# Finding a token's experts by comparing logits, with routing, early tokens and weight pieces in another order: a recurrence with a mixture of experts

## The chip, the core and the metric

The kernel runs on one core of one Trainium2 chip. The metric is the device time of one execution in microseconds (us). Three runs of the kernel before gave 386.06, 385.2 and 385.53, a median of 385.53. What a chip measurement here can tell from no change is about 0.2% of that. "TensorE" is PE in the profile, "VectorE" DVE, "ScalarE" ACT, "GpSimd" POOL and "SyncE" SP.

## What is computed

Inputs are `x` (2 x 1024 x 256), a start state per sequence, the recurrence's weights, a gate of 8 experts and three weight matrices for each of them. In the module, a recurrence over 64-step segments, then a mixture of experts, are added to `x`:

```python
xW = jnp.einsum('ntd,dh->nth', x, Wx) + b
next_h = jnp.tanh(xw_t + prev_h @ Wh)          # step by step
...
logits = x_flat @ gate_w.T                     # 2048 tokens, 8 experts
top_v, top_i = jax.lax.top_k(logits, 2)
probs = softmax(top_v)
hidden = silu(x_flat @ wg[e].T) * (x_flat @ wu[e].T)
out += weight[e] * (hidden @ wd[e].T)          # every expert e
```

Only the two experts with the largest logits have a weight other than zero for a token, so the kernel computes those alone.

## The kernel before, in words

**Tokens.** The 2048 hidden states are held as 16 tiles of 128 tokens (`r` = 0 to 15). The recurrence is not run over 64 serial steps of two sequences but in a wide form, 128 columns in each of the steps `s` = 8 to 63 (lines 623 to 670), whose warm-up the last part of the run checks: `chunk_starts` (line 550) subtracts the states where two chunks meet, `starts_check` (684) turns the differences into a mark `okh`, and `starts_flag` (677) adds it up over the partitions. If the mark fails, `stepwise` (1024) computes everything again, step by step, behind a branch at the end of the kernel. Steps 48 to 63 each finish one token tile.

**A step of the recurrence.** TensorE does four fp32 products (line 630) onto an accumulator that was *seeded* two steps earlier with `x @ Wx + b` (`seed`, line 315: one half copied by VectorE, one by ScalarE for s of 50 and more), then ScalarE does two tanh.

**Routing.** It is interleaved with steps 49 to 63, by a list of due times: `at(t, f)` files `f` under a time and `run(t)` (lines 556 to 562) carries out, in order of due times, everything due. `run` is called in the middle of step `s` with `s - 0.5` (line 629) and at its end with `s` (670), then in the main loop with `64 + n` plus a fraction. Every engine executes what it is given in program order, so a due time is a place in the queue of each engine that the function uses. The tiles are routed in four groups (`GROUPS = (5, 3, 5, 3)`). For a tile, `route_tile` (360) has TensorE transpose the states to rows with the logits behind them and ScalarE copy them to SBUF; `route_max` (370) takes the eight largest logits and their indices on VectorE. For a group, in this order:

- `route_choice` (376): one-hot rows `oh` of the two experts by comparing a counter with the indices, their sum `sel`, and the difference `dl` of the two logits. `route_weight` (394): tanh of `dl` on ScalarE.
- `rows_out` (389): the rows go to a DRAM table `rows_d` by SyncE's DMA queue.
- `route_position` (399): TensorE counts with small fp16 products (line 408) how many earlier tokens chose each expert. It reads `sel`.
- `route_code` (412): VectorE turns the count into a slot number, split into `v` and `m`. GpSimd puts the expert weights into the rows (464, 465).
- `route_onehot` (435), in three parts: two one-hot matrices (parts 0 and 2) and a multiplication by the token number (part 1). In the trace their tile is called `wd`, since they lie in that buffer.
- `route_slots` (449): TensorE multiplies them (line 455), so that a table says for every slot of every expert which token stands in it.

`early_gap` (430) and `early_slots` (481) need groups 0 and 1 only: GpSimd gathers the first two tiles of expert 0's tokens from `rows_d` (line 469) while the recurrence still runs, and `early_turn` (492) transposes them (line 216), splits them into a high part `xhi` on ScalarE and a low part `xlo` on VectorE. `all_slots` (495) does the rest after group 3.

**Experts.** `jobs` are experts, `units` are up to 512 token columns of one. Each unit takes `NIC` = 8 steps, numbered `n` through all units. In step `n` (lines 937 to 974) `front` (837) has TensorE do 12 products, gate first, then up, each as high x high, low x high, high x low (`products`, 722); `gate` (858) does silu on ScalarE and the product on VectorE, then splits the hidden values; `back` of step `n - 2` (877) does the second matmul (line 892) into `yb`. After a unit's last `back`, ScalarE scales its rows into `y` and GpSimd scatters them with an add. `turn` (822) transposes and splits the next unit's tokens. Weights of the next expert are loaded in fp32 by SyncE (771) and split into two parts in six pieces (`piece`, 773; ScalarE for the high part, VectorE for the low), at the places that `split_at` lists (927 to 933). `expert_order` (504) sorts the experts in five portions, one at each `next(order_ops)`.

Of the kernel before, what the change touches and what calls it, by code (L numbers as in the profile page):

```python
# [8 lines left out]
F32 = mybir.dt.float32  # L9
# [3 lines left out]
U32 = mybir.dt.uint32  # L13
# [6 lines left out]
P = 128  # L20
# [4 lines left out]
E = 8  # L25
# [11 lines left out]
NA = 8  # L37
ET = 2
TOL = 2.0**-18


class Pools:
# [15 lines left out]
def rnn_moe(ctx, tc, xT, xrows, h0T, Wx, Wh, b, gw, W, out):  # L58
# [282 lines left out]
    gi5 = ov.tile([P, NO * NS], I32, name="gi5")  # L341
    si5 = ov.tile([P, NO * NS], I32, name="si5")
    gap = ov.tile([P, 1], F32, name="gap")
    eq = ov.tile([P, NO * NS], F32, name="eq")
    sel = ov.tile([P, R, E], F16, name="sel")
    hot_space = spare[1].bitcast(F16)
# [13 lines left out]
    def route_tile(gr, r):  # L360
        i = r - gr["r0"]
        if i == 0:
            gr["mx"] = rt.tile([P, gr["n"], 8], F32, name="mx")
            gr["mi"] = rt.tile([P, gr["n"], 8], U32, name="mi")
        pt = ptr_tile()[:, 0:ROW]
        for k in range(2):
            pe(nc.tensor.matmul(pt[:, k * P : (k + 1) * P + E], lhsT=hall[k][:, r, :], rhs=ig[:, k, :], start=(k == 0), stop=(k == 1), skip_group_check=True))  # L367
        act.copy(gr["rows"][:, i, :], pt)

    def route_max(gr, r):  # L370
        i = r - gr["r0"]
        lg = gr["rows"][:, i, P : P + E]
        vec.max(gr["mx"][:, i, :], lg)
        vec.max_index(gr["mi"][:, i, :], gr["mx"][:, i, :], lg)

    def route_choice(gr):
        n = gr["n"]
        gr["oh"] = oh = rt.tile([P, n, 2, E], F32, name="oh")
        vec.tensor_tensor(
            oh,  # L380
            iota_f[:, 0:E].unsqueeze(1).unsqueeze(1).to_broadcast([P, n, 2, E]),
            gr["mi"][:, :, 0:2].unsqueeze(3).to_broadcast([P, n, 2, E]),
            ALU.is_equal,
        )
        vec.tensor_tensor(sel[:, gr["r0"] : gr["r0"] + n, :], oh[:, :, 0, :], oh[:, :, 1, :], ALU.add)
        gr["dl"] = dl = rt.tile([P, n], F32, name="dl")
        vec.tensor_tensor(dl, gr["mx"][:, :, 1], gr["mx"][:, :, 0], ALU.subtract)

    def rows_out(gr, cs):
        a, b = gr["r0"] * P, (gr["r0"] + gr["n"]) * P  # L390
# [21 lines left out]
    def route_code(gr):  # L412
        n = gr["n"]
        rows = route_rows(gr)
        tmp = rt.tile([P, n, 2, E], F32, name="tmp")
        next(rows)
        vec.tensor_tensor(tmp, gr["oh"], pos_ps[:, 0:n, :].unsqueeze(2).to_broadcast([P, n, 2, E]), ALU.mult)
        code = rt.tile([P, n, 2], F32, name="code")
        next(rows, None)
        vec.tensor_reduce(code, tmp, AX.X, ALU.add)  # L420
        big = 1.5 * 2.0**23 * P
        vv = rt.tile([P, n, 2], F32, name="vv")
        vec.tensor_scalar(vv, code, 0.5 - P / 2, big, ALU.add, ALU.add)
        gr["v"] = v = rt.tile([P, 2 * n, 2], F16, name="v")
        twice = lambda t: t.rearrange("p i c -> p (i c)").unsqueeze(2).to_broadcast([P, 2 * n, 2])
        vec.tensor_scalar(v, twice(vv), -big, 1.0 / P, ALU.add, ALU.mult)
        gr["m"] = m = rt.tile([P, 2 * n, 2], F16, name="m")
        vec.scalar_tensor_tensor(m, v, -float(P), twice(code), ALU.mult, ALU.add)

# [126 lines left out]
    def at(step, f, *args):  # L556
        todo.setdefault(step, []).append(lambda: f(*args))

    def run(step):
        for t in sorted(t for t in todo if t <= step):  # L560
            for f in todo.pop(t):
                f()
# [8 lines left out]


    maxima = {r: r + 49.5 for r in range(R)}
    maxima.update({5: 55, 8: 58.2, 9: 59.2, 10: 60.3, 11: 61, 13: 62.3, 14: 63.2, 15: 64.13})
    for g, gr in enumerate(groups):
        for r in range(gr["r0"], gr["r0"] + gr["n"]):
            at(r + 49 if r < 15 else 64.1, route_tile, gr, r)
# [2 lines left out]
    def group(g, choice, weight, position, code, hot, slots):  # L580
        gr = groups[g]
        at(choice, route_choice, gr)
        at(weight, route_weight, gr)
        at(choice + 0.01, rows_out, gr, ((0, P), (P + E, ROW)))
        at(position, route_position, gr)
        at(code, route_code, gr)
        at(code, rows_out, gr, ((P, P + E),))
        for part, t in enumerate(hot):
            at(t, route_onehot, gr, part)
        for i in range(gr["n"]):  # L590
            at(slots, route_slots, gr, i)

    group(0, 53.5, 53.6, 54.5, 54.5, (54.6, 54.6, 55.1), 57.1)
    group(1, 56.5, 56.6, 57, 57, (57.1, 57.1, 57.1), 59)
    at(57.6, early_gap)
    at(59, early_slots)
    group(2, 61.5, 61.6, 62, 62, (62.4, 63.3, 64.2), 66.6)
    at(62.1, early_turn)
    group(3, 64.13, 64.14, 65.1, 65.13, (65.2, 66.2, 67.2), 67.6)
    at(67.6, all_slots)  # L600
    at(69.6, chunk_starts)

    inj = {}
# [80 lines left out]
    def starts_check():  # L684
        vec.tensor_tensor(df, df, df, ALU.mult)
        vec.tensor_scalar(df, df, TOL * TOL, None, ALU.is_le)
        vec.tensor_reduce(okm, df, AX.XYZ, ALU.min)
        vec.tensor_copy(okh, okm)

    def loop_tile(pool, rank, kth):  # L690

# [27 lines left out]
    with ExitStack() as c2:  # L719
        open_late_pools(c2)  # L720

        def products(lhs_rhs, pt=None):

            if pt is None:
                pt = pgu_tile()
            for i, j in ((0, 0), (1, 0), (0, 1)):
                for n, (a, b) in enumerate(lhs_rhs):
                    pe(nc.tensor.matmul(  # L728
                        pt, lhsT=a[i], rhs=b[j],
                        start=(i + j + n == 0), stop=(j == 1 and n == len(lhs_rhs) - 1), skip_group_check=True))  # L730
            return pt

        def gated(pg, pu, between=lambda: None):
# [52 lines left out]
        class Unit:  # L786
# [49 lines left out]

            def front(u, s, between=lambda: None):

                w, x = u.job.w, u.x
                if u.main:  # L840
                    c = slice(s * P, (s + 1) * P)
                    n = u.cols
                    if 2 * n <= 512:
                        t = pgu_tile()
                        pt = [t[:, 0:n], t[:, n : 2 * n]]
                    else:
                        pt = [pgu_tile()[:, 0:n] for _ in range(2)]
                    pairs = [[(pick(w[nm], k, c), pick(x, k, slice(0, n))) for k in range(2)] for nm in NAMES[:2]]
                    pg = products(pairs[0], pt[0])
                    between()  # L850
                    pu = products(pairs[1], pt[1])
                else:
                    c = slice(s * 512, (s + 1) * 512)
                    a = slice(0, P)
                    pg, pu = (products([(pick(x, k, a), pick(w[nm], k, c)) for k in range(2)]) for nm in NAMES[:2])
                u.hid[s] = pg, pu
# [70 lines left out]
        split_at = {}  # L927
        for j in range(len(jobs) - 1):
            two = sum(u.job is jobs[j] for u in units) > 1
            for n, m in enumerate((2, 3, 4, 6, 7) if not two else (8, 10, 12, 14, 15) if j == 0 else (3, 4, 7, 10, 12, 15)):  # L930
                split_at[j, m] = j + 1, n
            if j == 0 or not two:
                split_at[j + 1, 0] = j + 1, 5
# [3 lines left out]
        for n in range(len(steps)):  # L937
            i, s = steps[n]
            u = units[i]
            j = jobs.index(u.job)  # L940
            m = s + (NIC if i and units[i - 1].job is u.job else 0)
            u.front(s, lambda: run(64 + n + 0.1))
            run(64 + n + 0.15)
            low = []

            def beside():
                run(64 + n + 0.2)
                if (j, m) in split_at:
                    to, p = split_at.pop((j, m))
                    low.append(jobs[to].piece(p, jobs[to + 1] if to + 1 < len(jobs) else None))  # L950

            u.gate(s, beside)
            for f in low:
                f()
            run(64 + n + 0.3)
            if n == 16:
                starts_check()
            elif n == 20:
                next(order_ops, None)
                starts_flag(ptr_tile()[:, 0:1])  # L960

            if n == 4:
                units[1].gather()
                units[2].gather()
            if s == (6 if i == 0 else 5) and i + 1 < len(units):
                units[i + 1].turn()
            for _ in range({5: 1, 6: 1, 7: 2, 9: 1}.get(n, 0)):
                next(order_ops)
            if i > 0 and s == 2 and i + 2 < len(units):
                units[i + 2].gather()  # L970
            if 2 <= n < len(steps) - NIC + TAIL + 2:
                v, t = units[steps[n - 2][0]], steps[n - 2][1]
                v.back(t)
            run(64 + n + 0.6)
# [183 lines left out]
```

## Time and profile before

| | us |
|---|---|
| three runs, median | 385.53 (385.2 to 386.06) |
| the profiled execution, its own time | 389.46 |
| its span, first to last instruction | 387.3 |
| TensorE busy in the span | 369.7 |
| recurrence and routing: first expert product (line 728) starts | 76.82 |
| first unit's last step's products start | 94.47 |
| second expert's first products start | 115.74 |

The span is divided in the view by stages as follows (length of the stage, then busy us of each engine with instruction counts, granted TensorE clock, share of DMA, GB/s):

```
0.00:28.00 28.00, 26.71 (x228) 25.36 (x228) 21.14 (x79) 15.26 (x57) 19.39 (x38) 1.00 0.81 301
28.00:53.00 25.00, 23.42 (x169) 20.24 (x168) 15.86 (x49) 15.51 (x52) 0.37 (x9) 1.00 0.37 127
53.00:76.80 23.80, 22.20 (x227) 21.69 (x226) 16.19 (x95) 16.33 (x61) 3.89 (x8) 1.00 0.23 59
76.80:98.20 21.40, 19.45 (x180) 18.59 (x178) 14.57 (x53) 7.37 (x21) 6.40 (x8) 1.00 0.34 89
98.20:128.50 30.30, 29.13 (x210) 27.11 (x210) 22.14 (x47) 17.87 (x36) 12.15 (x10) 1.00 0.48 146
128.50:175.00 46.50, 46.50 (x325) 43.54 (x325) 28.34 (x52) 23.60 (x44) 20.34 (x16) 1.00 0.51 137
175.00:372.00 197.00, 196.70 (x1344) 187.48 (x1343) 108.29 (x194) 99.81 (x188) 48.02 (x32) 1.00 0.33 81
372.00:387.40 15.40, 5.62 (x48) 5.39 (x46) 0.00 (x0) 1.90 (x4) 6.10 (x4) 0.83 0.31 36
```

The columns of engines are PE, PEld (weight loads, beside PE), DVE, ACT and POOL. Almost all VectorE and ScalarE operations carry one line number (L54, the helper that records them), so they are told apart by their tiles. A bracket at the end of a timeline row is the idle time of that engine before the row, and after the arrow who ended it.

### The profile page before, as it was taken

To read this page: it belongs to the slowest core of one execution; us is meant where nothing else is said; L and a number is where in the kernel's file an instruction comes from. 1 tells how busy PE (TensorE), PEld (TensorE's weight loads), DVE (VectorE), ACT (ScalarE), POOL (GpSimd) and SP (SyncE) were. 2 spreads that over 40 slices of the span, in tenths; PEclk is the share of its full clock that TensorE was granted. 3 is DMA by queue.
4 is the path that set the end of the run, shared out by engine and by line. 5 is a ranking of instruction groups with operands and counts; after the bars stand their busy time and mean duration, and the time that the engine had idled before them with its cause. 6 is when DMAs were issued, how large, how long until landed. Compare 5 with 4: busy or idle time off the path is not lost.

```text
span 387.3 us, 7245 instructions
## 1 busy us (share of the span) xinstructions
PE 369.7 (95%) x2717; PEld 349.4 (90%) x2717; DVE 226.5 (58%) x567; ACT 197.6 (51%) x458; POOL 116.7 (30%) x124
## 2 busy tenths in 40 slices
PE   8999999989999899999999999999999999999990
PEld 8998898889997789999999999999989999999890
DVE  6876648684777566564546564566545655663410
ACT  3746666632564644645445644665454555444420
POOL 3780001206171510783223602523040014006042
PEclk9999999999999999999999999999999999999997
DMA  7952334133075534664246243445143144003113
GB/s 223 460 202 96 108 111 114 50 95 82 5 191 181 135 111 135 151 199 89 86 125 126 72 129 94 81 138 135 30 107 114 47 173 51 1 2 40 13 20 38
DMA packets 19227, 42.20 MB, mean 109 GB/s; under 512 B 4802, under 2 KB 14178, under 8 KB 16066
## 3 DMA queue, kind: packets, MB, share of 16 engines
q1 hardware_dynamic: 12402, 32.32, 24.1%
q0 software_dynamic: 6496, 9.09, 14.3%
q8 instruction: 23, 0.38, 0.4%
q10 hardware_dynamic: 288, 0.26, 0.2%
q14 instruction: 18, 0.15, 0.1%
HBM read 35.15 MB, written 9.14 MB: 114 GB/s over the span
## 4 chain that ended last, share of the span: by engine, by line
PE 85%; DVE 4%; ACT 3%; DMA 2%; POOL 2%; issue 2%; SPq 1%; POOLq 0%; ACTq 0%; DVEq 0%
PE pgu_t L728 46%; PE yb L892 22%; PE pgu_t L630 8%; PE ptr L309 3%; PE ptr L216 2%; POOL out_dram L476 2%; DVE wd L54 1%; DMA wh<-in_Wh_dram 1%; PE pgu_t L892 1%; DMA xg<-rows_d,gidx 1%; PE ptr L641 1%; ACT h L54 1%; PE ptr L367 1%; PE ptr L892 1%; DVE g L54 1%
## 5 line engine op out<-in xcount | busy, mean ns | idle before, releaser
L892 PE MATMUL yb<-wd,hh 128*128 128x256 f32 (+2 forms) x544 | 94.3, 284 | 1.5 <-ACT y L54 1.5
L54 DVE TENSOR_TENSOR g<-g,pgu_t 128x256 f32<-128x256 f32 (+5 forms) x96 | 50.2, 522 | 64.1 <-PE pgu_t L728 44.3
L892 PEld LDWEIGHTS yb<-wd,hh 128*128 128x128 f32 (+2 forms) x544 | 80.4, 185 | 3.8 <-ACT y L54 2.2
L54 ACT ACTIVATE g<-pgu_t 128x256 f32<-128x256 f32 (+5 forms) x96 | 44.9, 468 | 71.3 <-PE pgu_t L728 66.1
L476 POOL DMA_INDIRECT out_dram<-y,si x27 | 44.1, 1635 | 119.5 <-ACT y L54 114.0
L728 PE MATMUL pgu_t<-xhi,gu_g 128*128 128x256 f32 (+5 forms) x384 | 78.3, 325 | 0.8 <-ACT xhi L54 0.8
L54 ACT CAST hh<-g 128x256 fp32r<-128x256 f32 (+5 forms) x92 | 44.7, 486 | 65.2 <-DVE g L54 62.5
L728 PE MATMUL pgu_t<-xhi,gu_u 128*128 128x256 f32 (+5 forms) x384 | 78.0, 325 | 0.0
L728 PEld LDWEIGHTS pgu_t<-xhi,gu_u 128*128 128x128 f32 x384 | 61.3, 188 | 4.3
L728 PEld LDWEIGHTS pgu_t<-xhi,gu_g 128*128 128x128 f32 x384 | 58.7, 189 | 3.3 <-ACT xhi L54 1.0
L54 DVE TENSOR_TENSOR hl<-g,hh 128x480 fp32r<-128x480 f32 (+4 forms) x52 | 31.1, 597 | 32.1 <-ACT hh L54 31.4
L892 PE MATMUL yb<-wd,hl 128*128 128x256 f32 (+1 forms) x176 | 49.6, 282 | 0.0
L728 PE MATMUL pgu_t<-xlo,gu_g 128*128 128x256 f32 (+5 forms) x192 | 46.7, 324 | 0.0
L728 PE MATMUL pgu_t<-xlo,gu_u 128*128 128x256 f32 (+5 forms) x192 | 46.5, 323 | 0.0
L469 POOL DMA_INDIRECT xg<-rows_d,gi x27 | 29.3, 1084 | 47.8 <-DVE cm L819 18.8
L728 PEld LDWEIGHTS pgu_t<-xlo,gu_g 128*128 128x128 f32 x192 | 32.5, 188 | 2.5 <-DVE xlo L54 0.2
L728 PEld LDWEIGHTS pgu_t<-xlo,gu_u 128*128 128x128 f32 x192 | 32.5, 188 | 2.2
L892 PEld LDWEIGHTS yb<-wd,hl 128*128 128x128 f32 (+1 forms) x176 | 32.2, 183 | 0.1
L630 PE MATMUL pgu_t<-h,wh 128*128 128x128 f32 (+1 forms) x224 | 28.6, 266 | 1.4
L54 DVE TENSOR_TENSOR hh<-g,hh 128x256 fp32r<-128x256 f32 x40 | 17.0, 426 | 20.5 <-ACT hh L54 18.8
L54 ACT ACTIVATE h<-pgu_t 128x128 f32<-128x128 f32 (+1 forms) x72 | 17.6, 277 | 13.7 <-PE pgu_t L630 8.4
L476 POOL DMA_INDIRECT out_dram<-y,sidx x8 | 13.2, 1650 | 30.6 <-ACT y L54 29.0
(161 smaller groups left out, 464.2 us busy)
## 6 DMA issues: line engine op xcount, KB each, us to landing
raw<-in_W_dram SPq DMA_DIRECT2D x24, 1024.0 KB, 4.8
gu_u<-in_xT_dram SPq DMA_DIRECT2D x6, 256.0 KB, 6.1
rows_d<-gu_u SPq DMA_DIRECT2D x4, 320.0 KB, 2.7
rows_d<-gu_u SPq DMA_DIRECT2D x4, 192.0 KB, 2.4
out_dram<-in_xrows_dram SPq DMA_DIRECT2D x1, 512.0 KB, 15.2
xg<-rows_d,gi POOLq DMA_INDIRECT x27
out_dram<-y,si POOLq DMA_INDIRECT x27
gu_u<-in_xT_dram ACTq DMA_DIRECT2D x2, 128.0 KB
```

Source lines behind the costliest of these rows:

```text
L54: return lambda *a, **k: self.tc.keep_in_program_order(f(*a, **k))
L216: pe(nc.tensor.transpose(pt[:, m, j, :], tiles[i][:, k * (P + E) : k * (P + E) + P], ident))
L309: pe(nc.tensor.matmul(pt, lhsT=l, rhs=r, start=(i == 0), stop=(i == len(ops) - 1)))
L367: pe(nc.tensor.matmul(pt[:, k * P : (k + 1) * P + E], lhsT=hall[k][:, r, :], rhs=ig[:, k, :], start=(k == 0), stop=(k == 1), skip_group_ch ...
L469: nc.gpsimd.indirect_dma_start(out=xg, out_offset=None, in_=rows[:, :], in_offset=bass.IndirectOffsetOnAxis(ap=idx, axis=0),)
L476: return nc.gpsimd.indirect_dma_start(out=out[:, :], out_offset=bass.IndirectOffsetOnAxis(ap=idx, axis=0), in_=y, in_offset=None, compute_ ...
L630: pe(nc.tensor.matmul(acc[s % 2][j], lhsT=w[:, k, j * P : (j + 1) * P], rhs=prev[k], start=False, stop=True, skip_group_check=True))
L641: pe(nc.tensor.matmul(pt, lhsT=zl, rhs=zl, start=True, stop=True))
L728: pe(nc.tensor.matmul(pt, lhsT=a[i], rhs=b[j], start=(i + j + n == 0), stop=(j == 1 and n == len(lhs_rhs) - 1), skip_group_check=True))
L892: pe(nc.tensor.matmul(yt[0:w, :], lhsT=h[a][:, i * P : i * P + w], rhs=wd[b][:, ic, :], start=(ic == 0 and first and n == 0), stop=(ic == ...
```

## The change

A tile's experts are no longer found by index. `route_max` keeps the eight largest logits alone, and `route_choice` compares the logits themselves with the largest two. Where two of the three largest logits are equal this would mark the wrong experts, so a new column of `tie` notes the token; a noted token shifts the rounding constant `big` in `route_code`, and at the end `starts_check` joins `tie` to the mark that sends the kernel to `stepwise`. Due times of the routing's parts, of the early tokens and of the weight pieces are others. The first front of the first unit does the products with `xhi` for gate and up ahead of those with `xlo`. `units[1].turn()` is placed before the gate of step 6, not after it.

```diff
     def route_max(gr, r):
-        lg = gr["rows"][:, i, P : P + E]
-        vec.max(gr["mx"][:, i, :], lg)
-        vec.max_index(gr["mi"][:, i, :], gr["mx"][:, i, :], lg)
+        vec.max(gr["mx"][:, i, :], gr["rows"][:, i, P : P + E])
...
         vec.tensor_tensor(
             oh,
-            iota_f[:, 0:E].unsqueeze(1).unsqueeze(1).to_broadcast([P, n, 2, E]),
-            gr["mi"][:, :, 0:2].unsqueeze(3).to_broadcast([P, n, 2, E]),
+            gr["rows"][:, :, P : P + E].unsqueeze(2).to_broadcast([P, n, 2, E]),
+            gr["mx"][:, :, 0:2].unsqueeze(3).to_broadcast([P, n, 2, E]),
             ALU.is_equal,
         )
-        vec.tensor_tensor(sel[...], oh[:, :, 0, :], oh[:, :, 1, :], ALU.add)
+        vec.tensor_tensor(sel[...], oh[:, :, 0, :], oh[:, :, 1, :], ALU.max)
         gr["dl"] = dl = rt.tile([P, n], F32, name="dl")
         vec.tensor_tensor(dl, gr["mx"][:, :, 1], gr["mx"][:, :, 0], ALU.subtract)
+        eq2 = rt.tile([P, n, 2], F32, name="eq2")
+        vec.tensor_tensor(eq2, gr["mx"][:, :, 0:2], gr["mx"][:, :, 1:3], ALU.is_equal)
+        bad = tie[:, gr["r0"] : gr["r0"] + n]
+        vec.tensor_reduce(bad, eq2, AX.X, ALU.max)
+        gr["big"] = big = rt.tile([P, n], F32, name="big")
+        vec.tensor_scalar(big, bad, 256.0 * P, BIG, ALU.mult, ALU.add)
...
-        vec.tensor_scalar(vv, code, 0.5 - P / 2, big, ALU.add, ALU.add)
+        vec.scalar_tensor_tensor(vv, code, 0.5 - P / 2, gr["big"].unsqueeze(2).to_broadcast([P, n, 2]), ALU.add, ALU.add)
...
-    maxima.update({5: 55, 8: 58.2, 9: 59.2, 10: 60.3, 11: 61, 13: 62.3, 14: 63.2, 15: 64.13})
+    maxima.update({5: 55, 8: 58, 9: 59, 10: 60, 11: 61, 13: 62.3, 14: 63.2, 15: 64.13})
...
-    group(0, 53.5, 53.6, 54.5, 54.5, (54.6, 54.6, 55.1), 57.1)
-    group(1, 56.5, 56.6, 57, 57, (57.1, 57.1, 57.1), 59)
-    at(57.6, early_gap)
-    at(59, early_slots)
+    group(0, 53.5, 53.6, 54.5, 54.5, (54.6, 56.2, 57.9), 59.5)
+    group(1, 56.5, 56.7, 57, 57, (57.1, 57.1, 58), 59.9)
+    at(58.1, early_gap)
+    at(59.9, early_slots)
     group(2, 61.5, 61.6, 62, 62, (62.4, 63.3, 64.2), 66.6)
-    at(62.1, early_turn)
-    group(3, 64.13, 64.14, 65.1, 65.13, (65.2, 66.2, 67.2), 67.6)
-    at(67.6, all_slots)
+    at(62.5, early_turn)
+    group(3, 64.13, 64.14, 65.12, 65.13, (65.2, 66.2, 67.2), 68.15)
+    at(68.15, all_slots)
...
-        vec.tensor_copy(okh, okm)
+        vec.tensor_reduce(tie[:, 0:1], tie, AX.X, ALU.max)
+        vec.scalar_tensor_tensor(okh, tie[:, 0:1], 0.0, okm, ALU.is_equal, ALU.mult)
...
+                    if u is units[0] and s == 0:
+                        for ab, p in zip(pairs, pt):
+                            products(ab, p, ((0, 0), (1, 0)), ab is pairs[0])
+                        between()
+                        for ab, p in zip(pairs, pt):
+                            products(ab, p, ((0, 1),))
+                        pg, pu = pt
...
-(8, 10, 12, 14, 15) if j == 0 else (3, 4, 7, 10, 12, 15)
+(6, 9, 10, 11, 14) if j == 0 else (3, 4, 7, 10, 12, 15)
...
+            if n == 6:
+                units[1].turn()
...
-            if n == 16:
+            if n == 17:
                 starts_check()
...
-            if s == (6 if i == 0 else 5) and i + 1 < len(units):
+            if i > 0 and s == 5 and i + 1 < len(units):
                 units[i + 1].turn()
-            for _ in range({5: 1, 6: 1, 7: 2, 9: 1}.get(n, 0)):
+            for _ in range({5: 2, 7: 2, 8: 1}.get(n, 0)):
                 next(order_ops)
```

The numbers in `group(...)` are the due times of choice, weight, position, code, the three one-hot parts, and slots. `products` takes the terms to do as a new argument.

More of the change, by code (lines that the diff above doesn't have):

```diff
@@ L39 @@
 TOL = 2.0**-18
+BIG = 1.5 * 2.0**23 * P
 class Pools:
@@ L343, in rnn_moe @@
     gap = ov.tile([P, 1], F32, name="gap")
+    tie = ov.tile([P, R], F32, name="tie")
     eq = ov.tile([P, NO * NS], F32, name="eq")
@@ L363, in route_tile @@
             gr["mx"] = rt.tile([P, gr["n"], 8], F32, name="mx")
-            gr["mi"] = rt.tile([P, gr["n"], 8], U32, name="mi")
         pt = ptr_tile()[:, 0:ROW]
@@ L380, in route_choice @@
             oh,
-            iota_f[:, 0:E].unsqueeze(1).unsqueeze(1).to_broadcast([P, n, 2, E]),
-            gr["mi"][:, :, 0:2].unsqueeze(3).to_broadcast([P, n, 2, E]),
+            gr["rows"][:, :, P : P + E].unsqueeze(2).to_broadcast([P, n, 2, E]),
+            gr["mx"][:, :, 0:2].unsqueeze(3).to_broadcast([P, n, 2, E]),
             ALU.is_equal,
         )
-        vec.tensor_tensor(sel[:, gr["r0"] : gr["r0"] + n, :], oh[:, :, 0, :], oh[:, :, 1, :], ALU.add)
+        vec.tensor_tensor(sel[:, gr["r0"] : gr["r0"] + n, :], oh[:, :, 0, :], oh[:, :, 1, :], ALU.max)
         gr["dl"] = dl = rt.tile([P, n], F32, name="dl")
         vec.tensor_tensor(dl, gr["mx"][:, :, 1], gr["mx"][:, :, 0], ALU.subtract)
+        eq2 = rt.tile([P, n, 2], F32, name="eq2")
[4 more added lines that the diff above has]
+        vec.tensor_scalar(big, bad, 256.0 * P, BIG, ALU.mult, ALU.add)
     def rows_out(gr, cs):
@@ L420, in route_code @@
         vec.tensor_reduce(code, tmp, AX.X, ALU.add)
-        big = 1.5 * 2.0**23 * P
         vv = rt.tile([P, n, 2], F32, name="vv")
-        vec.tensor_scalar(vv, code, 0.5 - P / 2, big, ALU.add, ALU.add)
+        vec.scalar_tensor_tensor(vv, code, 0.5 - P / 2, gr["big"].unsqueeze(2).to_broadcast([P, n, 2]), ALU.add, ALU.add)
         gr["v"] = v = rt.tile([P, 2 * n, 2], F16, name="v")
         twice = lambda t: t.rearrange("p i c -> p (i c)").unsqueeze(2).to_broadcast([P, 2 * n, 2])
-        vec.tensor_scalar(v, twice(vv), -big, 1.0 / P, ALU.add, ALU.mult)
+        vec.tensor_scalar(v, twice(vv), -BIG, 1.0 / P, ALU.add, ALU.mult)
         gr["m"] = m = rt.tile([P, 2 * n, 2], F16, name="m")
@@ L720, in rnn_moe, with products @@
         open_late_pools(c2)
-        def products(lhs_rhs, pt=None):
+        def products(lhs_rhs, pt=None, terms=((0, 0), (1, 0), (0, 1)), first=True):
             if pt is None:
                 pt = pgu_tile()
-            for i, j in ((0, 0), (1, 0), (0, 1)):
+            for i, j in terms:
                 for n, (a, b) in enumerate(lhs_rhs):
@@ L729, in products @@
                         pt, lhsT=a[i], rhs=b[j],
-                        start=(i + j + n == 0), stop=(j == 1 and n == len(lhs_rhs) - 1), skip_group_check=True))
+                        start=(first and i + j + n == 0), stop=(j == 1 and n == len(lhs_rhs) - 1), skip_group_check=True))
             return pt
@@ L848, in front @@
                     pairs = [[(pick(w[nm], k, c), pick(x, k, slice(0, n))) for k in range(2)] for nm in NAMES[:2]]
-                    pg = products(pairs[0], pt[0])
-                    between()
-                    pu = products(pairs[1], pt[1])
+                    if u is units[0] and s == 0:
[5 more added lines that the diff above has]
+                        pg, pu = pt
+                    else:
+                        pg = products(pairs[0], pt[0])
+                        between()
+                        pu = products(pairs[1], pt[1])
                 else:
@@ L929, in rnn_moe @@
             two = sum(u.job is jobs[j] for u in units) > 1
-            for n, m in enumerate((2, 3, 4, 6, 7) if not two else (8, 10, 12, 14, 15) if j == 0 else (3, 4, 7, 10, 12, 15)):
+            for n, m in enumerate((2, 3, 4, 6, 7) if not two else (6, 9, 10, 11, 14) if j == 0 else (3, 4, 7, 10, 12, 15)):
                 split_at[j, m] = j + 1, n
```

## The prediction

> **What bounds the kernel now.** I read the page first: busy shares, then the chain that ended last.
>
> ```profile
> PE 369.7 (95%) x2717; PEld 349.4 (90%) x2717; DVE 226.5 (58%) x567; ACT 197.6 (51%) x458; POOL 116.7 (30%) x124
> PE 85%; DVE 4%; ACT 3%; DMA 2%; POOL 2%; issue 2%; SPq 1%; POOLq 0%; ACTq 0%; DVEq 0%
> ```
>
> TensorE is the bound, and the diff removes no matmul. So the change can only be worth TensorE's idle time, and only where other engines are late. The view of waits, for TensorE from 53 to 178 us, lists all of it (us in total, times, longest):
>
> ```profile
> PE yb L892 <- ACT y L54: 1.5, 2, 1.2
> PE yb L408 <- DVE sel L54: 1.4, 2, 0.9
> PE pgu_t L728 <- ACT xhi L54: 0.8, 1, 0.8
> PE yb L455 <- DVE wd L54: 0.7, 1, 0.7
> PE pgu_t L216 <- DMA xg<-rows_d,gidx: 0.6, 1, 0.6
> ```
>
> The timeline of TensorE places them (start, duration, instruction, idle time before it):
>
> ```profile
> 65.78 0.17 PE L408 MATMUL yb<-sel,upper 128*128 128x24 f16 x1 [0.90 <-DVE sel L54]
> ...
> 75.51 0.55 PE L216 MATMUL pgu_t<-ident,xg 128*128 128x128 f32 x3 [0.58 <-DMA xg<-rows_d,gidx]
> ...
> 80.32 0.17 PE L408 MATMUL yb<-sel,upper 128*128 128x24 f16 x1 [0.47 <-DVE sel L54]
> ...
> 87.24 0.51 PE L455 MATMUL yb<-wd 128*128 128x128 f16 x6 [0.74 <-DVE wd L54]
> ...
> 97.51 0.73 PE L728 MATMUL pgu_t<-xhi,gu_g 128*128 128x256 f32 x4 [0.75 <-ACT xhi L54]
> ...
> 126.91 0.50 PE L892 MATMUL yb<-wd,hh 128*128 128x256 f32 x2 [1.17 <-ACT y L54]
> ```
>
> With 0.12 at 73.77 and 0.30 at 177.54 this is 5.0 us; nothing else idles until the last matmuls. That is the ceiling. Now each place.
>
> **Routing on VectorE.** Groups by form show what goes (count | busy, mean ns | idle before):
>
> ```profile
> L54 DVE MAX8 mx<-gu_u 128x8 f32<-128x8 f32 x16 | 2.6, 164 | 3.7 <-ACT gu_u L54 3.7
> L54 DVE FIND_INDEX8 mi<-mx,gu_u 128x8 uint32<-128x8 f32 x16 | 2.6, 160 | 0.0
> L54 DVE MATCH_VALUE_LOAD mi<-mx,gu_u 128x8 f32 x16 | 1.5, 92 | 0.6
> ```
>
> MAX8 at 77.32 is followed at 77.67 by the next independent operation: 0.35 us for the three, about 0.1 for a MAX8 alone when its successor doesn't need it (dl at 65.65 to the copy at 65.72: 0.07; sel to dl 0.10), 0.20 when it does. So 0.15 to 0.27 leaves per token tile, about 0.2 x 16 = 3.3 us of VectorE. Added per group: eq2, bad, big. Nearest rows are dl (161 ns) and the small reduce to code (203 ns): independent start 0.08, then two dependent ones at 0.22, about 0.5 x 4 = 2.0 us, all behind sel and dl, which are what others wait for. Comparing with logits instead of a counter, max for add, and scalar_tensor_tensor for vv (m, the same kind, 180 ns; vv now 214) cost nothing either way: same shapes. Most of this is cover already; what counts is when sel, the one-hots (wd) and the seeds come.
>
> **Group 1's positions (65.78).** VectorE just before:
>
> ```profile
> 62.91 0.41 DVE L54 TENSOR_TENSOR wd<-wd,tok 128x480 f16<-128x480 f16 x1
> ...
> 63.58 0.81 DVE L54 TENSOR_TENSOR wd<-iota,m 128x1280 f16<-128x1280 f16 x1
> ...
> 65.31 0.21 DVE L54 TENSOR_TENSOR oh<-iota_f,mi 128x48 f32<-128x48 f32 x1
> ...
> 65.55 0.18 DVE L54 TENSOR_TENSOR sel<-oh 128x24 f16<-128x24 f32 x1
> ```
>
> The 0.81 moves behind the choice, but the 0.41 (slot 56.2) still stands in front of it, and the seed copy ahead of that waits for ScalarE's tanh, which ends at 64.27. So seed 64.31, +0.20 one-hot, +0.32 MAX8, +0.20 oh, +0.24 sel, +0.18: ready at 65.45, matmul at 65.50 instead of 65.78. Gain 0.28; the other 0.6 stays. Bounds: 0 (eq2 and its two companions of group 0 push the chain) to 0.9.
>
> Seeds are the cover here: hot parts of groups 0 and 1 (0.73 + 0.47) now lie between the seeds of steps 60 and 61. Step 60's copy: 67.95 to 68.24, TensorE needs it near 68.46; step 61's 69.71 to 70.0, needed near 70.42. Margins of 0.2 and 0.4; without them the recurrence pays directly, up to 0.5.
>
> **Early tokens: a wait moves and grows.** Slots of group 1 go from 59 to 59.9, group 0's from 57.1 to 59.5. TensorE order is unchanged in amount (0.25 and 0.18 of L455), but the gathers of the early tokens hang on group 1's slots. Before: slots 69.14, gather issue 69.97 on POOL, second 71.46, transposes reached at 74.65. From slots to transposes 5.51. After: step 58 from 65.73, two steps of 1.36, 0.53 + 0.25 + 0.53 to slots at 69.77; from there to the transposes 0.18 + 0.47 + 0.89 + 0.47 + 0.89 + 0.47 + 0.52 + 0.53 = 4.42, at 74.19. The gather needs, from slots, 0.83 to issue and 1.49 to the second issue, then its landing. The chain says `71.46 4.00 DMA`, but of that gather's 16 landing marks fifteen are in by 74.26 (2.80) and one comes at 75.47. The Trainium skill, "DMA: Bandwidth & Descriptors", section "Anatomy of one DMA — SWDGE (gpsimd) path", puts a GpSimd-issued DMA at about 2.0 us plus bytes over 436e3: for 128 rows of 1,056 bytes 2.3 us, an estimate. It speaks against the later slots only a little (second tile at 74.4, wait 0.2); by the fifteen marks 74.89 (0.7); by the straggler 76.1 (1.9). I take 2.80, the bulk of the nearest row: transposes resume at 74.94. Against the profile's 75.51 that is -0.57; against a run without the straggler, where 74.65 had no wait, it is +0.29. What stands behind the waiting transposes on TensorE is all the rest, and on SP the `landed` DMA and group 2's row stores; these have 3 us of slack until the late gathers (rows landed 84.99, gather 88.24).
>
> **First front and group 3.** While the gather is awaited, VectorE stood idle for 1.23 before xlo (76.71); now the maxima of tile 13 and the first one-hot of group 2 (0.72) fill it, since early_turn goes behind them (62.5). Products with xhi for gate and up come before xlo's: about -0.1 (0.07 of gap at 77.46). Counted from the transposes' end: xlo 76.6, tile 14, second one-hot 0.65, tile 15's copy from ScalarE near 78.7, then 0.20 + 0.24 + 0.18: sel near 79.3. Its matmuls are issued one half later (65.12 is behind the up products), near 80.0: no wait. -0.6 (0.47 idle plus restart: 79.66 to 80.75 holds 0.43 of matmuls). Slots of group 3 pass front 4 (1.42): last one-hot done near 85.9, slots near 86.6, no wait: -0.85 (0.74 plus restart).
>
> **The late tokens' turn.** Slots to the second unit's transposes shrinks from 5.68 to 4.26 (back 0.71 + front 1.42, twice), while the gathers need 0.49 + 1.29 + 2.46 to 2.80, so 4.24 to 4.58: a wait of 0 to 0.35 where 1.3 of slack was, +0.2; 1.2 more if one mark straggles. xhi then goes ahead of front 6's silu on ScalarE, 5 us before its use: the 0.75 goes. That price is doubtful, since before the stall ScalarE shows
>
> ```profile
> 95.47 0.39 ACT L54 ACTIVATE g<-pgu_t 128x256 f32<-128x256 f32 x1 [2.75 <-PE ptr L216]
> ```
>
> though front 6 ended at 93.48: 2.0 us of delay for which I see no instruction, in the midst of six gathers. The same shows at 117.22 (front 15 ended at 115.19).
>
> **starts_check, weight pieces.** At 123.47 to 124.78 the check (0.42, 0.29, 0.42, 0.16) and a piece's 1.22 lay in front of g of front 17; hence hh at 125.50 and y at 126.03, 1.17 of TensorE. The check moves one step on and piece 4 to step 14; front 17's g then starts near 123.1, y ends near 125.3, TensorE comes at 125.7. -1.17. The check grows by about 0.2 (reduce for copy, and one more), under front 18's 2.8. Pieces at 9, 10, 11: VectorE 0.42 + 0.43 + 1.22 = 2.07 in a step of 2.13, ScalarE 0.39 + 0.41 + 1.04: fits. Steps 6 and 7 carry 2.5 and 2.4, a lag of 0.7 against 2.4 of slack before back(n) reads hl. Weights reach SP earlier (step 9 for 10), never later. Cost nothing; without that slack 0.7.
>
> **Sum.** In the profiled execution (389.46; span 387.3, 2.2 outside): -0.57 - 0.1 - 0.6 - 0.85 + 0.2 - 0.75 - 1.17 = -3.8. But it is 3.9 above the median 385.53, so some of its stalls are likely not in plain runs. The suspects are the straggler (0.86 between -0.57 and +0.29), 0.75 and 1.17. Without all three: -1.06. I count the last two half: -2.0, hence 383.5.
>
> **Rivals.** (a) All stalls of the profile are in plain runs: 381.7. For: the waits are plain semaphore waits. Against: the 3.9 us. Chance 0.2. (b) Gathers eat it: only VectorE's stalls go (-1.5) and both turns wait 0.7 each: 385.4, as much as no change (0.2%, 0.8 us, is what can be told apart). For: slack 1.3 and 0.4 both vanish. Chance 0.14. (c) Slower: gathers straggle in every run. The second early gather then takes 4.0 from 72.09, transposes at 76.1 instead of 74.65 with bulk landing before (+1.45), the late turn waits 1.2: 2.65 against 1.55 of gain, 386.6. It decides once a gather lands 0.9 later than 2.80 while before it had hidden. A late seed would add to it. Chance 0.19. (d) Likeliest as above, 383.5, own range 382.2 to 384.7: chance 0.47. The change certainly does what it says to VectorE; that this doesn't reach TensorE is (b).
>
> Faster 0.67, same 0.14, slower 0.19. The range leaves out the ends of (a) and (c): 381.3 to 386.2.
>
> **What would show it.** Right: TensorE's waits for sel fall to one near 65.5 with about 0.6; none for wd, xhi or y; transposes L216 wait 0.5 to 1.0 near 74.2 and a little near 91. Wrong: that wait over 1.5, a wait of L630 for a seed (DVE pgu_t), or a stall for y still at 125. It is wrong altogether if plain runs had none of the stalls.

## The result, and the profile after

The changed kernel takes 383.93 us (median of 7, 383.44 to 384.74) against 385.78 (7 runs, 385.07 to 386.2): ratio 0.9957, 95% interval 0.9943 to 0.997, 1.7 us less. 383.5 had been forecast, "faster", with 381.3 to 386.2 as range.

The page of the changed kernel (384.74 us in its profiled execution), with busy shares and the head of the chain that ended last:

```profile
PE 367.7 (96%) x2717; PEld 348.8 (91%) x2717; DVE 224.2 (59%) x548; ACT 197.9 (52%) x458; POOL 118.0 (31%) x124
PE 89%; DMA 3%; POOL 2%; ACT 1%; DVE 1%; issue 1%; SPq 1%; POOLq 0%
```

The number of matmuls is the same 2717; VectorE has 19 instructions fewer (32 searches out; four times three new operations and one in the check in). TensorE's waits between 53 and 200 us, the view that was five lines long before, are two, both for gathered tokens:

```profile
PE pgu_t L217 <- DMA xg<-rows_d,gidx: 1.0, 1, 1.0
PE ptr L217 <- DMA xg<-rows_d,gidx: 0.4, 1, 0.4
```

and the timeline of TensorE places them (L217 is line 216 of before):

```profile
74.99 0.79 PE L217 MATMUL pgu_t<-ident,xg 128*128 128x128 f32 x4 [1.03 <-DMA xg<-rows_d,gidx]
...
92.01 0.55 PE L217 MATMUL ptr<-ident,xg 128*128 128x128 f32 x3 [0.35 <-DMA xg<-rows_d,gidx]
```

Waits for sel, wd, xhi and y are gone: in this profile no engine's arithmetic holds TensorE up in this stretch any more, only the landing of gathers does. (In two later profiles of the same order of work a wait for y of 0.3 to 0.4 is left, near 172 us.) The view of before's profile needs a caution, though. Its execution took 389.46 us, 3.7 above the median now, and the experiments show that it was not a typical one. Between two typical profiles of one session, of before (385.67 us) and of the changed kernel (383.91), the chain moves less than the 85% to 89% that the first pair of pages suggests:

```profile
PE 89%; POOL 3%; DVE 2%; issue 2%; ACT 1%; DMA 1%; POOLq 0%; DVEq 0%; ACTq 0%
PE 92%; DMA 2%; POOL 2%; ACT 1%; issue 1%; DVE 0%; POOLq 0%
```

### The profile page after: what moved, and what is told of

Same layout as the page of the kernel before. It is cut to its first block, busy times and chain, and to the rows that moved or that the text cites. A ratio compares the mean times of both kernels' runs of the same rounds, so it can differ in the third digit from the quotient of the medians.

```text
span 382.7 us, 7225 instructions
## 1 busy us (share of the span) xinstructions
PE 367.7 (96%) x2717; PEld 348.8 (91%) x2717; DVE 224.2 (59%) x548; ACT 197.9 (52%) x458; POOL 118.0 (31%) x124
## 4 chain that ended last, share of the span: by engine, by line
PE 89%; DMA 3%; POOL 2%; ACT 1%; DVE 1%; issue 1%; SPq 1%; POOLq 0%
PE pgu_t L735 48%; PE yb L908 23%; PE pgu_t L636 10%; PE ptr L310 2%; DMA xg<-rows_d,gidx 2%; PE ptr L217 2%; POOL out_dram L482 2%; PE ptr L368 2%; DMA wh<-in_Wh_dram 1%; PE pgu_t L908 1%; PE ptr L647 1%; ACT h L55 1%; PE ptr L908 1%; DVE pgu_t L55 0%; PE yb L461 0%
## 5 line engine op out<-in xcount | busy, mean ns | idle before, releaser
L475 POOL DMA_INDIRECT xg<-rows_d,gi x27 | 30.9, 1144 | 54.7 <-DVE cm L826 19.8
L636 PEld LDWEIGHTS pgu_t<-h,wh 128*128 128x128 f32 x152 | 18.4, 190 | 4.2 <-ACT h L55 3.3
```

Source lines behind the costliest of these rows:

```text
L475: nc.gpsimd.indirect_dma_start(out=xg, out_offset=None, in_=rows[:, :], in_offset=bass.IndirectOffsetOnAxis(ap=idx, axis=0),)
L636: pe(nc.tensor.matmul(acc[s % 2][j], lhsT=w[:, k, j * P : (j + 1) * P], rhs=prev[k], start=False, stop=True, skip_group_check=True))
```

## The experiments

Three sessions measured groups of kernels, each with before beside them on the same chip: before took 390.6 in the first, 385.8 in the second, 388.9 in the third, so kernels are compared within a session. Some expectations below speak of chips that differ; the record gives chip number 2 for the first and the second session and 4 for the third, so the number of the chip does not tell the sessions apart. Two theories were set against each other. A: the gain that counts everywhere is VectorE being out of TensorE's way in the routing; the waits for xhi and y belong to some sessions only, where ScalarE hears late from TensorE while gathers follow one another. B: all stalls of the first profile are the kernel's own, and the main loop's new order gives much of the gain.

**Before once more.** No edit.

> The kernel before, unchanged, for a second profile. Theory A (the first profile holds stalls that a typical run hasn't: it took 389.46 us, the median is 385.8): this profile takes about 386, TensorE waits for sel (near 65.8 and 80.3) and for wd (87) as before, about 2.1 us of idle time, but not for xhi at 97.5 nor for y at 126.9, and ScalarE's 2.0 us delay at 95.5 is gone. Theory B (all stalls are of the kernel): the waits for xhi (0.75) and y (1.17) are there again. Ratio 1.000 in both.

389.83 (10 runs), ratio 1.0002 (0.9976 to 1.0029). The expected 386 did not come, and B's stalls did; ScalarE's row before the wait for xhi:

```profile
92.80 0.41 ACT L54 CAST hh<-g 128x256 fp32r<-128x256 f32 x1 [0.49 <-issue]
95.99 0.38 ACT L54 ACTIVATE g<-pgu_t 128x256 f32<-128x256 f32 x1 [2.79 <-remote]
```

The same pause as in the first profile (2.75 there), with TensorE stalled for 0.80 (xhi) and 1.28 (y) after it. Whether a typical run has it stayed open.

**Before in another session.** No edit; one execution, in the second session.

> Before once more, for its profile on this chip. Theory A: if it takes about 385.8, no wait for xhi at 97.5 and none over 0.3 for y at 127; if about 390, both. The waits for sel and wd are there on either.

385.67 us. The waits of TensorE, 53 to 200 us:

```profile
PE yb L408 <- DVE sel L54: 1.4, 2, 0.9
PE pgu_t L216 <- DMA xg<-rows_d,gidx: 0.8, 1, 0.8
PE yb L455 <- DVE wd L54: 0.8, 1, 0.8
```

No xhi, no y; and ScalarE's timeline at the same step, where silu starts 0.86 after the operation before it instead of 2.8:

```profile
91.82 0.41 ACT L54 CAST hh<-g 128x256 fp32r<-128x256 f32 x1 [0.49 <-DVE g L54]
93.08 0.38 ACT L54 ACTIVATE g<-pgu_t 128x256 f32<-128x256 f32 x1 [0.86 <-PE pgu_t L728]
94.10 0.41 ACT L54 CAST hh<-g 128x256 fp32r<-128x256 f32 x1 [0.63 <-DVE g L54]
```

One program, two profiles, 4.5 us apart, and stalls that only the longer one has: A as to where they belong. The waits for sel and wd are in both, to 0.01 us. The two stalls are not the whole difference, though: the stretches that hold them are 1.0 us (second front to ninth) and 1.5 us (seventeenth to twenty-fifth) longer, and of the rest 1.25 us lies ahead of the first routing product, 0.4 us between the ninth front and the seventeenth and 0.7 us behind the twenty-fifth (the routing itself is 0.3 us shorter). (A front is the twelve first products of a step in the main loop; it is counted from its start.)

**The main loop's part alone**, on before:

```diff
-(8, 10, 12, 14, 15) if j == 0
+(6, 9, 10, 11, 14) if j == 0
+            if n == 6: units[1].turn()
-            if n == 16:  starts_check()
+            if n == 17:  starts_check()
-{5: 1, 6: 1, 7: 2, 9: 1}
+{5: 2, 7: 2, 8: 1}
```

> Before, with the main loop's part alone: the second unit's turn ahead of gate 6, starts_check at step 17, pieces at 6, 9, 10, 11, 14, expert order at 5, 5, 7, 7, 8. Theory A: it removes stalls that typical runs don't have, so 385.6 to 386.0, ratio 0.999 to 1.001. Theory B: the 0.75 and 1.17 go, 383.9, ratio 0.995: then this part alone is the gain measured.

388.95 against 390.64, ratio 0.9959 (0.9938 to 0.9981): as B expected, in a session where before has these stalls. y's wait (1.28) is gone, xhi's stays (0.84), although the turn is ahead of the gate. By the two profiles the part saves 1.5 us from the seventeenth front to the twenty-fifth, where y's wait was, and loses 1.0 us from the ninth to the seventeenth (19.32 against 18.29), where silu of the eighth to fifteenth fronts starts 1.1 to 2.9 us after the end of its front (0.1 to 1.7 in the repeat of before). That is 0.5 us net, and 0.8 with all stretches from the first routing product on, where the medians differ by 1.7; the rest is not placed (this profile, 387.89, is the shortest of its twelve runs).

**The due times and the first front alone**, on before: the `maxima`, `group`, `early_...` and `products` lines of the diff.

> Before, with the due times of routing and early tokens and the split first front; indices are still found. Theory A: the choice of group 1 comes 1.2 us earlier on VectorE (two one-hot parts behind it), group 3's wait for sel and wd go, the early transposes wait about 1 us for their gather: about 384.6, ratio 0.997. Theory B: no more than 0.3 us, ratio 0.999, the early gather's wait eating the rest.

387.28, ratio 0.992 (0.989 to 0.995), more than A expected. Waits:

```profile
PE yb L901 <- ACT y L54: 1.8, 2, 1.4
PE pgu_t L216 <- DMA xg<-rows_d,gidx: 0.5, 1, 0.5
PE ptr L216 <- DMA xg<-rows_d,gidx: 0.3, 1, 0.3
```

With the index searches still in place, sel and wd have left the list, and with them xhi. ScalarE's pause is still there, but it falls one step later, behind the operation that makes xhi. y remains.

```profile
92.58 0.58 ACT L54 CAST xhi<-ptr 128x512 fp32r<-128x512 f32 x1
96.22 0.39 ACT L54 ACTIVATE g<-pgu_t 128x256 f32<-128x256 f32 x1 [3.06 <-remote]
```

**Logits alone**, on before, all due times kept: `route_max`, `route_choice`, `big`, `tie`.

> Before, with experts found by comparing logits alone, all due times as before. Theory A: VectorE reaches group 1's sel about 0.5 us earlier (three index searches and those of group 0 before it, less the three new operations) and group 3's about 0.5, its last one-hot about 0.6: TensorE gains 1.0 to 1.5, ratio 0.9965. Theory B: VectorE time isn't on the path, 0.999 to 1.000.

387.94, ratio 0.9939 (0.9918 to 0.9959).

```profile
PE yb L899 <- ACT y L55: 1.7, 2, 1.3
PE pgu_t L735 <- ACT xhi L55: 0.8, 1, 0.8
PE yb L461 <- DVE wd L55: 0.8, 1, 0.8
PE pgu_t L217 <- DMA xg<-rows_d,gidx: 0.7, 1, 0.7
```

sel is off the list here too; wd isn't. So either half is enough for the two waits for sel, and only the due times remove wd. The parts save 1.7, 3.4 and 2.7 us by their medians, 7.8 together, and overlap: they can't be added. Logits and due times were measured apart in the first session alone, the one with the added stalls; how the gain divides between them in a session like the second was not measured.

**The changed kernel again**, and **without the main loop's part** (those lines as in before, the rest changed), second session:

> The changed kernel, unchanged, beside before on one chip. The first measurement (383.9 against 385.8) and the parts (where before took 390.6) are of chips that differ by 5 us. Theory A (where several gathers follow one another, ScalarE and VectorE hear late from TensorE on some chips and not on others, and the changed main loop hides that): where before takes about 390.5, this takes 384.5 to 385.5, ratio 0.985 to 0.987; where before takes about 385.8, 383.9, ratio 0.9955. Theory B (the gain is the same everywhere): 0.9955 on both.

> The changed kernel with the main loop's part as it was before (turn after gate 6, check at 16, pieces at 8, 10, 12, 14, 15). Theory A: on a chip where before takes 390.5 it waits for y again and is 1.3 to 1.9 us slower than the changed kernel; where before takes 385.8, within 0.4 us of it. Theory B: 1.6 slower on both.

383.91 (ratio 0.9957, 0.9943 to 0.997) and 383.80 (0.995, 0.9936 to 0.9963), before 385.80. Without the main loop's part the kernel is as fast, as A expected. Its waits:

```profile
PE pgu_t L217 <- DMA xg<-rows_d,gidx: 1.2, 1, 1.2
PE ptr L217 <- DMA xg<-rows_d,gidx: 0.5, 1, 0.5
```

the same two as in the changed kernel (0.9 and 0.5 there).

**The changed kernel a third time**, third session:

> The changed kernel beside the three others. Where before takes 385.8: 383.9, ratio 0.9955. Where before takes 390.5: theory A (its main loop hides the late news from TensorE) 385, 0.986; theory B 388.8, 0.9955.

384.44 against 388.93: ratio 0.9893 (0.9876 to 0.9909). This is A, in size a little off (0.986 had been for a before of 390.5). Over the sessions before moves by 4.8 us, the changed kernel by half a microsecond, as far as they met. It was not run in the first session, and before was not profiled in the third. The changed kernel's third profile does show that the session has the pause and that TensorE no longer waits for it: the eighth front ends at 93.71 and ScalarE's silu starts 1.70 us later, against 0.10 us in the second session, yet the stretch from the second front to the twenty-fifth takes 67.68 us against 67.77. Its half microsecond lies behind the twenty-fifth front (218.83 against 218.27).

```profile
95.41 0.38 ACT L55 ACTIVATE g<-pgu_t 128x256 f32<-128x256 f32 x1 [1.67 <-remote]
```

**Room for both gathers**, second session, on the changed kernel:

```diff
-at(62.5, early_turn)                 # route_tile of r = 15 at 64.1
+at(63.1, early_turn)                 # ... at 63.15
-            if n == 6: units[1].turn()      ahead of the gate
+            if n == 6: units[1].turn()      behind back(4)
```

> The changed kernel with room for both gathers: slots of group 1 and the early gathers half a step earlier (59.55), the early turn behind step 63 and tile 15's product right behind it, the late turn behind the back of step 6. Theory A: the 1.0 us wait for the early gather and the 0.35 for the late one go, 1.0 to 1.5 us faster than the changed kernel. Theory B (the early turn is limited by something else that follows, xhi on ScalarE or the first front): 0 to 0.3 faster.

384.19, ratio 0.9954 (0.994 to 0.9968): no gain. Waits:

```profile
PE pgu_t L735 <- DVE xlo L55: 1.0, 1, 1.0
PE pgu_t L735 <- ACT xhi L55: 0.3, 1, 0.3
```

Both waits for gathers have gone, and one of 0.97 for xlo came. VectorE's timeline tells why:

```profile
93.19 1.22 DVE L55 TENSOR_TENSOR gu_g<-raw,gu_g 128x1024 fp32r<-128x1024 f32 x1
94.32 0.68 DVE L55 TENSOR_TENSOR xlo<-ptr,xhi 128x512 fp32r<-128x512 f32 x1
```

The weight piece of step 6 stands ahead of xlo. In the changed kernel the turn is ahead of the gate, so xlo is ahead of the piece. The last run below supports this: with the first piece at step 8 the wait for xlo is gone.

**Three more in the third session.** Slots at 59.55 for 59.9; the same with the early turn as above and the late turn as in the changed kernel; and the run before this with the first piece at step 8 for 6.

> The changed kernel with slots of group 1 and the early gathers at 59.55 in place of 59.9. Theory A (the wait at the early transposes is the gather's length counted from the slots): the gather is issued 0.4 to 0.5 us earlier and TensorE's wait falls by as much, 0.9 to 0.5: about 0.4 us faster than the changed kernel. Theory B (the last landing mark comes at a time of its own, near 75, whatever the issue): no gain.

> As the run before, and the early turn behind step 63 with tile 15's product behind it; the late turn as in the changed kernel. From the earlier run with both turns moved, whose first part was 0.4 us faster up to the fifth front and whose later part lost 1.0 to xlo: 0.4 us faster than the changed kernel, late turn's wait of 0.5 unchanged. Theory B: within 0.1, since xhi then bounds the first front.

> Both turns moved, and the first weight piece at step 8 in place of 6, so that its 1.22 us on VectorE no longer stand ahead of xlo. Theory A: the 0.97 wait for xlo goes and the late gather's 0.5 stays gone: 0.9 faster than the changed kernel, about 383.0 where before takes 385.8. Theory B: another wait (a piece later, y) takes it back, 0 to 0.3.

The first is a miss of mine: the middle of step 60 takes what is due by 59.5, so 59.55 waits for the step's end as 59.9 did, and every engine's order is that of the changed kernel. The same holds for the 59.55 in the run above and in the other two. It is a repeat (384.37 against 384.44) and tells the noise. Whether earlier slots help was not tried. The second took 383.92 against 384.44 with ranges that overlap (383.48 to 385.18, 383.71 to 385.47): undecided. Its early wait is 0.30 for xhi in place of 0.59 for the gather, and the late one stays. The third took 385.16, ratio 0.9907 (0.9892 to 0.9922): B's another wait, and worse. Neither late tokens nor xlo are waited for. From the ninth to the seventeenth front TensorE took 19.6 us, against 17.9 in the changed kernel, with this on its timeline:

```profile
102.45 1.20 PE L908 MATMUL yb<-wd,hh 128*128 128x256 f32 x6 [0.39 <-ACT hh L55]
```

Pieces now stand in four steps running (8 to 11), and silu of the eleventh front starts 3.7 us after the front's end, against 1.95 us in the changed kernel, both in the third session. That the four pieces leave no step to catch up in is a reading of this; whether the order would lose as much in a session without ScalarE's pauses was not tried.

## Why the prediction was right, and where only its sum was

Starts of routing products and fronts in two typical profiles of the second session, before (385.67) and changed (383.91), give this:

| stretch of TensorE, us | before | changed | gain |
|---|---|---|---|
| first routing product to first front | 23.87 | 22.84 | 1.03 |
| first front to second | 2.14 | 1.97 | 0.17 |
| second front to ninth | 17.65 | 16.84 | 0.81 |
| ninth to seventeenth | 17.91 | 17.94 | -0.03 |
| seventeenth to twenty-fifth | 33.10 | 32.99 | 0.11 |
| from there to the last front's end | 218.27 | 218.27 | 0.00 |

2.09 in all, 1.89 by the medians of that session. (Ahead of the first routing product the changed kernel's profile is 0.26 longer.)

- **What bounds it**: right. TensorE's idle time, with the restart behind each wait, was the ceiling, and the gain lies where waits went: the last stretch, without any, gains 0.00.
- **Group 1's positions, 0.28**: mis-sized. All 0.90 went. The failed step is "the seed copy ahead of that waits for ScalarE's tanh, which ends at 64.27": the copy belongs to a tanh one step earlier. In the changed profile it stands at 63.64, and there the first routing product came 0.47 later than in the first profile, so 63.17 on the old clock:

```profile
63.64 0.29 DVE L55 COPY pgu_t<-hl 128x128 f32<-128x128 f32 x1 [0.16 <-ACT gu_g L55]
...
64.48 0.17 DVE L55 MAX8 mx<-gu_u 128x8 f32<-128x8 f32 x1 [0.24 <-ACT gu_u L55]
...
64.93 0.18 DVE L55 TENSOR_TENSOR sel<-oh 128x24 f16<-128x24 f32 x1
```

  sel is ready at 65.11, TensorE's product starts at 65.20 and waits for nothing:

```profile
65.20 0.17 PE L415 MATMUL yb<-sel,upper 128*128 128x24 f16 x1
```

- **Seeds between the moved one-hots**: the margins held; no wait of the recurrence in any profile.
- **Early tokens, a wait that grows**: it did, to 0.6 to 1.0 in the four profiles with the changed kernel's order, where 0.75 was worked out, but not as worked out. The 0.75 was the second gather's fifteenth mark (its landing is counted in 16 marks, see the last section). In the changed profile that mark is in at 74.57; TensorE resumes at 74.99, 0.13 behind the last mark of the *first* gather (74.86). So the size was met for another reason. And "against a run without the straggler, where 74.65 had no wait, it is +0.29" failed. No such run was found: every profile of before has a wait there (0.58, 0.47, 0.76). So the stretch that holds group 1's positions and the early tokens gained 1.03 and didn't lose 0.29; about 1.05 of it is the wait for sel with its restart (1.31 to 0.26 from the group's first counting product to the next step of the recurrence).
- **First front 0.1, group 3's 0.6 and 0.85**: right. 0.17 in the second row; the third holds 0.81 net of the late turn, which cost 0.68 (0.48 of wait and the restart), so about 1.5 gross.
- **Late tokens' turn, 0.2**: a wait of 0.35 to 0.48, and 0.57 to 0.68 with the restart, so mis-sized by a factor of three. The term that was too small is the second late gather's landing: "2.46 to 2.80" from its issue, where the profiles of the changed kernel with all its marks show 2.94 (89.03 to 91.97) and 3.07 (88.03 to 91.10).
- **xhi and y, 0.75 and 1.17, counted half**: the doubt was right and the half was not. In the session of 385.8 they gave nothing that can be told from zero (383.91 against 383.80 without the main loop's part); in that of 390.6 the same part gave 1.7 us by itself, by the medians. The step "I count the last two half: -2.0" put in 0.96 that this measurement hadn't, and the late turn cost 0.4 to 0.5 more than the sum had; the stretch with group 1 and the early tokens gained 1.3 more than the sum had. The forecast of 383.5 came within 0.5 of the 383.93 by luck in this part: an error of about 1.4 one way and one of 1.3 the other nearly cancel.

Rival (a), all stalls in plain runs, holds for the first session's before, whose profile has them all; in the third the whole gain was 4.5 us, but its 381.7 was never reached. (b) had the two waits right in sum (0.93 and 0.48 for 0.7 each), but before waits for the early gather as well (0.76), so its 385.4 was missed. (c) had its mechanism right, a straggling mark, but it was there before as well.

## What to carry to other kernels

Compare the profiled execution's own time with the median before reading its stalls: here one was 3.7 us above it, and 2 us of the stalls that it showed were of the session. When several queues stand between a cause and a wait, two different edits may each remove the whole wait, so parts measured alone overlap. And a step moved to cover one latency should be read on every engine that it is queued on: the turn that made room for a gather put xlo behind a weight piece.

## What the runs showed of the hardware

**One late landing mark.** A gather counts 16 marks. In each of the fourteen profiles the last mark of one of the two early gathers comes 1.0 to 1.7 us after the mark before it, and a packet of 16 KB on an instruction queue has just been moved. The late mark follows the packet's end by nearly the same time, 1.24 to 1.30 us, in all fourteen, whichever gather it belongs to. From the traces' landing marks and packets, five of them:

| profile | gather | last mark but one on record, last mark | packet starts, takes | packet's end to last mark |
|---|---|---|---|---|
| before, 385.67 | second | 73.66, 74.96 | 72.31, 1.40 | 1.25 |
| logits alone | second | 72.91, 73.89 | 71.57, 1.09 | 1.24 |
| due times alone | first | 73.27, 74.50 | 71.98, 1.22 | 1.30 |
| changed, 384.74 | first | 73.33, 74.86 | 72.63, 0.95 | 1.28 |
| without the main loop's part | first | 72.42, 74.09 | 71.35, 1.46 | 1.28 |

The packet in the view of DMA of the changed kernel, 71 to 76 us (queue, kind: packets, MB, share of 16 engines), with the landing of the two gathers:

```profile
q0 software_dynamic: 96, 0.27, 19.5%
q8 instruction: 1, 0.02, 1.2%
...
xg<-rows_d,gidx POOLq DMA_INDIRECT x2, 3.9
```

That the packet shares a DMA engine with one sixteenth of the gather is an inference; no run was made to move the packet. But if the late mark belongs to the packet, issuing a gather a little earlier would not bring its last mark earlier, which speaks for theory B of the run with slots at 59.55. The 2.3 us estimated from the Trainium skill ("DMA: Bandwidth & Descriptors", "Anatomy of one DMA — SWDGE (gpsimd) path") is exceeded by 2.2 by the last mark of the changed kernel's first gather and by 0.6 by its fifteenth (gather issued at 70.39, marks at 74.86 and 73.33).

**ScalarE hears late.** In before's profiles of 389.46 and 390.14 ScalarE resumes 2.0 us and more after the products that it waited for by TensorE's records, amid six gathers in a row (and again amid seven at 110 to 119); in that of 385.67 it resumes 0.1 after. No instruction lies in between in either. What differs between the sessions was not found and stays open. One difference is in the traces themselves: of about 1,985 landing marks that the profiles of the second session hold, the one of 389.46 holds 1,649, those of the first session 1,612 to 1,652 and those of the third 1,678 to 1,687. The profiles with ScalarE's pauses are those with marks missing. Whether the recording of the trace slows the cores in these sessions, or one cause does both, no run shows.
